# Stages of the last two images issued beside the mixture ahead of each, in a four-layer scan and attention kernel

## The chip, the cores and the metric

The kernel runs on one core of a Trainium2 chip. A core has five engines with queues of their own: TensorE (PE, matmuls into PSUM), VectorE (DVE), ScalarE (ACT, table functions), GpSimd (POOL) and SyncE (SP, which issues DMAs). Each engine takes its instructions in the order in which the program emitted them. The metric is device time in microseconds: 6460.27 as the median of three runs, from 6456.73 to 6466.56.

## The reference

Input and output are four images of 1024 tokens with 256 channels, in float32. Four layers follow each other:

```python
x = conv_scan_block(x)              # layer 0: projection to 512, 3x3 depthwise conv, gelu,
                                    #   scan with 64 states, layernorm, projection; + x
x = bottleneck_conv(x)              # layer 1: 1x1, grouped 3x3, 1x1; relu(out + x)
t = t + graph_attention(_ln_t(t))   # layer 2: masked attention over 1024 tokens, 8 heads,
t = t + moe2(_ln_t(t))              #   mixture of 8 experts, top 2, hidden 256
t = t + scan_block(_ln_t(t))        # layer 3: scan with 16 states over 512 channels,
t = t + moe3(_ln_t(t))              #   mixture of 8 experts, top 2, hidden 512
```

The scan is `h[t] = exp(dt[t] * A) * h[t-1] + dt[t] * x[t] * B[t]`, `y[t] = sum over states of C[t] * h[t]`, for each channel and state, along the 1024 tokens of an image. In both mixtures every expert is computed for every token and weighted by a coefficient that is zero for six of the eight.

## The kernel before

Eight scans (layer 0 or 3, image 0 to 3) run one after the other in the order of `SCANS`: (0,0), (0,1), (3,0), (0,2), (3,1), (0,3), (3,2), (3,3). A scan is cut into units of 128 rows of (state, channel) by 1024 tokens: 256 units for a scan of layer 0, 64 for one of layer 3. One unit is made by `scans`: a DMA of the step sizes dt, spread over the states (`load`, tile dA); `exp(A dt)` on ACT in place (`decay`); two bf16 matmuls that spread the input, held as three bf16 parts in tile S, over the states (`first`, ps_rep); on VectorE a product with the row B and `tensor_tensor_scan`; on POOL a product with the row C; and for each pair of units four matmuls that sum over the states (`pair`, ps_y), which are copied and stored once for 64 channels. A scan's 512 channels are four groups d of 128; each has its own tile S, fetched by `chunk` about `AHEAD = 12` units before its first unit.

All else is in stages that are generators: `front` (layer 0 up to its scan), `middle` (rest of layer 0, layer 1, attention, `moe(2)`, and `front3`, which is layer 3 up to its scan), and `last` (`back3`, which is layer 3 behind its scan, and `moe(3)`). A stage yields a cost after each small step. `run` advances the scans by half a unit and then, with a clock per engine that adds up modelled costs, takes up to `TICKS = 2` steps of the current stage for as long as no engine's clock is ahead of VectorE's. So the two are interleaved in every engine's queue, in an order that is fixed when the program is written. Stages run one at a time, in the order of `STAGES`; `last` of image 2 comes after `middle` of image 3. A stage that needs a scan's result yields a `Wait`, and is taken up again when that group's y store has been emitted.

If the channels of the coming scan are not ready, `chunks_ahead` holds the scan back: with `LATEST = 5` units to go it calls `need`, which advances the stages and nothing else until they are. This happens ahead of scan (3,3), whose input comes from `middle` of image 3: four units of scan (3,2) are then still to be emitted.

The parts of a scan's input come from `steps`: a projection (ps_dt), softplus on ACT (Abs, Exp, Identity, Ln), a sum and a product, a split into three bf16 parts, and stores of dt and parts to DRAM, from where `load` and `chunk` fetch them. For the first scan of the kernel alone it takes another way, with `between`: two projections and softplus first, some other work, and then sums on VectorE, with the parts written from SBUF to S directly (`parts_direct`).

`moe` loads the weights of expert 0, normalizes, transposes, computes router logits (ps_lg), softmax and top 2 (`route`), adds the second bias (ps_b), and then pipes through blocks of one expert and 512 tokens: a group of matmuls ps_h for each 128 hidden channels, Gelu on ACT into h_m, two groups ps_e, and a multiply-add on VectorE into the residual tb. `pipe` issues the later step of one item ahead of the first step of the next. Three PSUM buffers go around for all stages (`ps`): a group waits until the reader of the group three before it is done. `back3` fetches the residual, the gate and y, multiplies y by the gate on POOL, and projects it (ps_o). `pipe`, and all engine calls inside `run`, are recorded at line 128, so that most rows of the profile carry L128.

Of the kernel before, what the change touches and what calls it, by code (L numbers as in the profile page):

```python
# [7 lines left out]
F32 = mybir.dt.float32  # L8
BF16 = mybir.dt.bfloat16
# [7 lines left out]
P = 128  # L17
NB = 4
L = 1024
TB = L // P  # L20
C = 256
# [3 lines left out]
NEXP = 8  # L25
# [16 lines left out]
AHEAD = 12  # L42
LATEST = 5


# [87 lines left out]
class Wait(tuple):  # L133
    pass


class Hybrid:
# [240 lines left out]
    def scans(self, mp, psum):  # L378
# [9 lines left out]
        for scan in SCANS:  # L388
            G = P // self.states[scan[0]]
            units += [  # L390
                (scan, d, c, i, j)
                for d in range(DC) for c in range(2) for i in range(32 // G) for j in range(2)
            ]
        chunks, rows, waiting = {}, {}, []
        state = {}
        self.scan_psum = psum
        y = None

        def load_rows(scan):
            bct, n = self.mem["bc", *scan], self.states[scan[0]]  # L400
            pair = []
            for t in range(2):
                x = mp.tile([P, L], F32, tag=f"rows{t}", name=f"rows{t}", bufs=2)
                nc.sync.dma_start(
                    x, bct[t * n : (t + 1) * n, :].unsqueeze(1).to_broadcast([n, P // n, L])
                )
                pair.append(x)
            rows[scan] = pair

        self.direct = mp.tile([3 * 32, 4, L], BF16, tag="S", name="S", bufs=2)  # L410

# [9 lines left out]
        def chunk(k):  # L421

            if k >= len(units):
                return
            scan, d, c, i, j = units[k]
            if (c, i, j) != (0, 0, 0):
                return
            self.need(scan, d)
            S = self.direct if k == 0 else mp.tile([3 * 32, 4, L], BF16, tag="S", name="S", bufs=2)
            if k == 0:  # L430
                parts_direct(range(1, 4), nc.sync)
            elif d == 0:
                load_rows(scan)
            if k:
                for s in range(3):
                    nc.sync.dma_start(
                        S[32 * s : 32 * s + 32, :, :],
                        self.mem["parts", *scan, d][s].rearrange("(j p) t -> p j t", p=32),
                    )
            chunks[scan, d] = S  # L440

        def chunks_ahead(k, late=False):

            if not late and k + AHEAD < len(units) and units[k + AHEAD][2:] == (0, 0, 0):
                waiting.append(k + AHEAD)
            while waiting:
                scan, d = units[waiting[0]][:2]
                if ("parts", *scan, d) not in self.ready:  # L450
                    if waiting[0] - k > LATEST:
                        break
                    if not late:
                        return True
                    self.alone = True
                chunk(waiting.pop(0))
                self.alone = False
            return False

        def load(k):  # L460
            if k >= len(units):
                return
            scan, d, c, i, j = units[k]
            n = self.states[scan[0]]
            G = P // n
            a = mp.tile([P, L], F32, tag="dA", name="dA", bufs=5)
            r = 64 * c + 32 * j + G * i
            nc.sync.dma_start(
                a, self.mem["dt", *scan, d][r : r + G, :].unsqueeze(0).to_broadcast([n, G, L])
            )  # L470
            state[k] = a

        def decay(k):
            if k >= len(units):
                return
            scan, d, c, i, j = units[k]
# [6 lines left out]
        def first(k):  # L483
            if k >= len(units):
                return
# [38 lines left out]

        self.load, self.load_rows, self.parts_direct = load, load_rows, parts_direct
        for k in range(AHEAD):
            chunk(k)
        for k in range(2, 4):
            load(k)
        decay(0)  # L530
        decay(1)
        first(0)
        for k in range(len(units) + 4):
            waits = chunks_ahead(k)
            load(k + 4)
            if not waits:
                first(k + 1)
            decay(k + 2)
            if k < len(units):
                a, inp = state.pop(k)  # L540
                B, Cm = rows[units[k][0]]
                nc.vector.tensor_tensor(inp, inp, B, ALU.mult)
            yield
            if k < len(units):
                h = mp.tile([P, L], F32, tag="h", name="h", bufs=5)
                nc.vector.tensor_tensor_scan(h, a, inp, 0.0, ALU.mult, ALU.add)
                nc.gpsimd.tensor_tensor(h, h, Cm, ALU.mult)
                state[k] = h
            if k % 2 == 1 and 2 <= k < len(units) + 2:
                pair(k - 2)  # L550
            if waits:
                chunks_ahead(k, True)
                first(k + 1)
            yield
# [68 lines left out]
    def steps(self, fp, key, w, src, chunks, bias, u, between=None):  # L623
# [65 lines left out]
        if between is not None:  # L689
# [6 lines left out]
            yield from between  # L696
            self.load_rows(key)
            for item in ahead:
                add(item, nc.vector)
            for item in ahead:  # L700
                split(item)
            self.load(0)
            self.load(1)
            for item in ahead:
# [876 lines left out]

    def moe(self, which, b, tb):

# [5 lines left out]
        KH = hidden // P  # L1589
        with tc.tile_pool(name=f"m{which}{b}", bufs=1, side="right") as op:  # L1590
            xT = op.tile([P, 2, L], F32, name="xTm")
            cw = op.tile([P, TB, NEXP], F32, name="cw")

# [6 lines left out]

            weights = {0: expert_weights(0)}
            with tc.tile_pool(name=f"mg{which}{b}", bufs=1, side="right") as gp:
                xn = gp.tile([P, TB, C], F32, name="xnm")
# [51 lines left out]
                yield from self.pipe(range(TB // 2), last, add, cost=1.0)  # L1655

            hidden_of = {}
            got = {}
# [105 lines left out]
    def front3(self, b, tb):  # L1764
# [3 lines left out]
        with tc.tile_pool(name=f"g{b}", bufs=1, side="right") as op:  # L1768
# [76 lines left out]
            with tc.tile_pool(name=f"gc{b}", bufs=1, side="right") as fp:  # L1845
                bct = fp.tile([2 * N, L], F32, name="bct3")

                def low(g):
# [6 lines left out]
                nc.sync.dma_start(self.keep(("bc", *key), [2 * N, L]), bct)  # L1855
                yield from self.steps(
                    fp, key, lambda k, d: w_dt[:, k, d * P : (d + 1) * P], u, DC,
                    vec["L3_attn_b_dt"], u,
                )

    def back3(self, b, tb):
        nc, tc = self.nc, self.tc
        with tc.tile_pool(name=f"h{b}", bufs=1, side="right") as sp:
            nc.sync.dma_start(tb, self.mem["t", b])
# [82 lines left out]
    def middle(self, b):  # L1947

        with self.tc.tile_pool(name=f"t{b}", bufs=1, side="right") as tp:
# [3 lines left out]
            yield from self.attention(b, tb)  # L1953
            yield from self.moe(2, b, tb)
            yield from self.front3(b, tb)

    def last(self, b):
        with self.tc.tile_pool(name=f"e{b}", bufs=1, side="right") as tp:
            tb = tp.tile([P, TB, C], F32, name="tb")
# [47 lines left out]
```

## Time and profile before

| | us |
|---|---|
| median of three runs | 6460.27 |
| profiled execution, as timed | 6467.21 |
| its span, first to last instruction | 6465.4 |
| PE busy | 5210.1 (81%) |
| DVE busy | 5153.1 (80%) |
| ACT busy | 3408.1 (53%) |
| POOL busy | 3648.4 (56%) |

Busy time is a sum over the execution; the forty slices and a table of stretches show where it lies. PE's end times are modelled. A row of a group of instructions gives its output and inputs by tile name, the shapes, the count, the busy time in us, the mean of one in ns, and the idle time of its engine just before it with what ended that. The chain of waits goes back from the last instruction to what released each, and its shares show what set the end. The granted PE clock was 0.825 of full speed over the whole span.

### The profile page before, as it was taken

What the parts mean: (1) busy time and instruction counts of PE and PEld (TensorE: products, weight loads), DVE (VectorE), ACT (ScalarE), POOL (GpSimd) and SP (SyncE); (2) the same over time, 40 slices, a digit from 0 to 9 for tenths busy, and PEclk for the clock granted to TensorE, in tenths of its full rate; (3) what the DMA queues carried; (4) which work ended last, traced back from release to release, by engine and by line L of the source; (5) the groups of instructions that cost most, each with busy time, mean ns of one, the idle gap of its engine ahead of it and who ended that gap; (6) DMA issues with size and microseconds to landing.
All of it is one profiled execution on the core that took longest, in us unless ns stands there. A gap on an engine that the chain in (4) does not pass through costs nothing. (4 is left out here: it accounts for less than half of the span.)

```text
span 6465.4 us, 59678 instructions
## 1 busy us (share of the span) xinstructions
PE 5210.1 (81%) x20249; PEld 2107.8 (33%) x20249; DVE 5153.1 (80%) x4328; ACT 3408.1 (53%) x4075; POOL 3648.4 (56%) x1796
## 2 busy tenths in 40 slices
PE   6677685689797579989689689798699688968979
PEld 2222130222342022243245232253254222524656
DVE  5888989988898998899889988898899981258311
ACT  3565664355576335567568445477387353246311
POOL 2797868665557666555856665557756661065100
PEclk7677695689797579989789689798699788978979
DMA  3555546443355566345644665354555750156221
GB/s 114 162 158 174 176 154 198 158 147 116 125 182 174 169 163 163 114 137 178 193 150 165 189 158 142 107 168 163 178 169 168 193 146 7 53 154 159 64 69 33
DMA packets 347995, 935.77 MB, mean 145 GB/s; under 512 B 37444, under 2 KB 119952, under 8 KB 346064
## 3 DMA queue, kind: packets, MB, share of 16 engines
q1 hardware_dynamic: 345248, 929.36, 47.2%
q0 software_dynamic: 2128, 2.13, 0.2%
q8 instruction: 166, 2.72, 0.2%
q14 instruction: 165, 1.35, 0.1%
q10 hardware_dynamic: 288, 0.20, 0.0%
HBM read 841.81 MB, written 93.16 MB: 145 GB/s over the span
## 5 line engine op out<-in xcount | busy, mean ns | idle before, releaser
L128 POOL TENSOR_TENSOR h<-h,rows 128x1024 f32<-128x1024 f32 x1280 | 3026.7, 2367 | 1816.9 <-DVE h L128 1567.0
L128 DVE TENSOR_TENSOR_SCAN h<-dA,ps_rep 128x1024 f32<-128x1024 f32 x1280 | 2923.0, 2284 | 142.8 <-ACT dA L128 12.8
L128 DVE TENSOR_TENSOR ps_rep<-ps_rep,rows 128x1024 f32<-128x1024 f32 x1280 | 1550.9, 1212 | 182.6 <-PE ps_rep L128 178.4
L128 ACT ACTIVATE dA<-dA,A_L_conv_A_log 128x1024 f32<-128x1024 f32 x1024 | 1147.7, 1144 | 616.5 <-DMA dA<-dt 575.9
L128 PE MATMUL ps_rep<-S,spread_L_conv_A_log 96*128 96x512 bf16 x2048 | 770.4, 465 | 840.8 <-DVE h L128 791.1
L128 PE MATMUL ps_y<-h,collect_L_conv_A_log 128*32 128x512 f32 x4096 | 739.5, 773 | 14.6 <-POOL h L128 14.6
L128 PE MATMUL ps_h<-xTm,we 128*128 128x512 f32 x1536 | 716.5, 606 | 0.0
L128 PE MATMUL ps_e<-we,h_m 128*128 128x256 f32 x3072 | 701.2, 381 | 2.5 <-ACT h_m L128 1.7
L128 PEld LDWEIGHTS <-spread_L_conv_A_log 96*128 96x128 bf16 x2048 | 159.3, 103 | 1651.4 <-DVE h L128 1348.1
L128 ACT ACT_TABLE_LOAD x483 | 619.7, 1283 | 58.4 <-PE ps_h L128 43.1
L128 PEld LDWEIGHTS ps_e<-we,h_m 128*128 128x128 f32 x3072 | 579.2, 190 | 153.6 <-issue 62.7
L128 DVE SCALAR_TENSOR_TENSOR tb<-ps_e,cw,tb 128x256 f32<-128x256 f32 x512 | 220.1, 474 | 410.6 <-PE ps_e L128 410.5
L128 ACT ACTIVATE h_m<-ps_h,cols 128x512 f32<-128x512 f32 x384 | 260.2, 687 | 507.7 <-PE ps_h L128 505.2
L128 ACT ACTIVATE p<-ps_sc 128x512 f32<-128x512 f32 x432 | 234.4, 595 | 382.8 <-PE ps_sc L128 381.9
L128 PEld LDWEIGHTS ps_h<-xTm,we 128*128 128x128 f32 x1536 | 292.4, 193 | 333.4 <-issue 287.8
L128 ACT ACTIVATE dA<-dA,A_L_attn_A_log 128x1024 f32<-128x1024 f32 x256 | 290.6, 1146 | 198.3 <-DMA dA<-dt 168.8
L128 PE MATMUL ps_rep<-S,spread_L_attn_A_log 96*128 96x512 bf16 x512 | 182.7, 444 | 178.6 <-DVE h L128 167.7
L128 PE MATMUL ps_at<-p,v 128*32 128x512 f32 x1024 | 276.6, 621 | 0.9 <-ACT sums L128 0.7
L128 PE MATMUL ps_at<-p,ones 128*32 128x512 f32 x1024 | 276.5, 620 | 0.0
L128 PE MATMUL ps_sc<-qT,kT 32*128 32x512 f32 x864 | 262.6, 665 | 14.8 <-ACTq L1382 8.8
L128 POOL TENSOR_TENSOR sp_l<-sp_l,sp_e 128x512 f32<-128x512 f32 x62 | 78.4, 1265 | 272.4 <-DVE sp_e L128 250.5
L128 PE MATMUL ps_cv<-pad,diag 128*128 128x512 f32 x504 | 230.9, 599 | 0.0
(333 smaller groups left out, 4926.2 us busy)
## 6 DMA issues: line engine op xcount, KB each, us to landing
dA<-dt SPq DMA_DIRECT2D x1280, 512.0 KB
we<-in_L_ffn_W_dram SPq DMA_DIRECT2D x64, 512.0 KB
parts<-parts SPq DMA_DIRECT2D x62, 384.0 KB
S<-parts SPq DMA_DIRECT2D x93, 256.0 KB
dt<-sp_r SPq DMA_DIRECT2D x64, 256.0 KB
y<-yo SPq DMA_DIRECT2D x128, 128.0 KB
y_back<-y SPq DMA_DIRECT2D x64, 256.0 KB
we<-in_L_ffn_w_dram SPq DMA_DIRECT2D x64, 256.0 KB
```

Source lines behind the costliest of these rows:

```text
L128: return got(*args, **kw)
```

## The change

1. The list of units gets `DRAIN = 4` empty units ahead of the last scan, and for that scan `chunks_ahead` holds back only with one unit to go. So all of scan (3,2), stores included, is emitted before `need` is called. Loads and decays are counted by `upto`, which stops at a unit whose parts are not fetched.
2. `middle` of image 3 creates `ahead(2)`, that is `back3(2)` and `moe(3, 2)` up to its router, in pools on the left side of SBUF. `beside` takes one step of it after each step of `moe(2, 3)`; `rest` runs what is left up to the marker `END`.
3. In `front3` of image 3, `steps` takes the way with `between`, which is here `BETWEEN = 8` steps of image 2's experts; their first weights are loaded at that point (`begin` of `moe`). The parts of the last scan's first channel group go directly into S, and two loads of dt and the rows are issued ahead. When that group is ready, `beside` adds a step of image 2's experts after each step of the other three groups.
4. `last(2)` runs the rest of image 2's experts with `ahead(3)` beside it, one step each; steps that wait for the last scan are left out until their group is done. `last(3)` is what remains, its expert weights again loaded behind the router.
5. B and C rows are one tile of two halves. Image 2's residual uses one of its buffers, its transposed tokens use the tile of image 0's input, and the bct of front3 of image 3 uses the tile of layer 0's input weights.

```diff
+DRAIN = 4
+BETWEEN = 8
...
+        final = next(k for k, unit in enumerate(units) if unit[0] == SCANS[-1])
+        units[final:final] = [None] * DRAIN
+        final += DRAIN
...
-            S = self.direct if k == 0 else mp.tile([3 * 32, 4, L], BF16, tag="S", name="S", bufs=2)
-            if k == 0:
+            if k in (0, final):
+                S = self.direct
                 parts_direct(range(1, 4), nc.sync)
...
-                    if waiting[0] - k > LATEST:
+                    if waiting[0] - k > (1 if waiting[0] == final else LATEST):
...
+        def upto(what, one, k):
+            while ahead[what] <= k:
+                to = unit(ahead[what])
+                if to and to[:2] not in chunks:
+                    break
+                if to:
+                    one(ahead[what])
+                ahead[what] += 1
...
-            load(k + 4)
+            upto("load", load, k + 4)
...
-            self.load_rows(key)
+            self.begin(key)
...
-            self.load(0)
-            self.load(1)
+            self.two_loads()
...
+            if pause:
+                yield END
+                begin()
...
-                    vec["L3_attn_b_dt"], u,
+                    vec["L3_attn_b_dt"], u, self.some(self.other, BETWEEN) if last else None,
                 )
+                if last:
+                    steps = self.beside(steps, self.other, lambda: ("parts", *key, 0) in self.ready)
+                yield from steps
...
-            yield from self.moe(2, b, tb)
+            moe = self.moe(2, b, tb)
+            if b < NB - 1:
+                yield from moe
+            else:
+                self.other = self.ahead(b - 1, "left", self.scan_pool)
+                yield from self.rest((yield from self.beside(moe, self.other)))
             yield from self.front3(b, tb)
...
+    def beside(self, main, other, begin=lambda: True):
+
+        held = None
+        for cost in main:
+            yield cost
+            if other is None or not begin() or (held and held not in self.done):
+                continue
+            held = None
+            more = next(other, END)
+            if more is END:
+                other = None
+            elif isinstance(more, Wait):
+                held = tuple(more)
+            else:
+                yield more
+        if held:
+            yield Wait(held)
+        return other
...
+    def ahead(self, b, side, pool=None):
+
+        with ExitStack() as stack:
+            if pool is None:
+                pool = stack.enter_context(self.tc.tile_pool(name=f"e{b}", bufs=2, side=side))
+            tb = pool.tile([P, TB, C], F32, tag="rows", name="tb_rows", bufs=2 if pool is self.scan_pool else 1)
+            yield from self.back3(b, tb, side)
+            yield from self.moe(3, b, tb, side, True)
+            self.nc.sync.dma_start(self.image(self.out, b), tb)
+            yield 1.0
+
     def last(self, b):
+        if b == NB - 2:
+            self.other, before = self.ahead(b + 1, "right"), self.other
+            yield from self.beside(before, self.other)
+            return
+        if b == NB - 1:
+            for more in self.other:
+                if more is not END:
+                    yield more
+            return
```

## The prediction

> **What bounds the kernel now.** I read the page's forty slices first, then a table of stages, then the chain of waits.
>
> ```profile
> PE   6677685689797579989689689798699688968979
> DVE  5888989988898998899889988898899981258311
> GB/s 114 162 158 174 176 154 198 158 147 116 125 182 174 169 163 163 114 137 178 193 150 165 189 158 142 107 168 163 178 169 168 193 146 7 53 154 159 64 69 33
> ```
>
> For 33 slices VectorE is 8 to 9 tenths busy: the scans set the pace, and the change leaves them alone there. It acts on the last seven slices, where VectorE falls to 1 or 2: first image 3 finishes its middle stages with no scan beside it, then the last scan runs, then two images finish one after the other. Cut at the trace's own borders (columns: stretch, length, then busy time and count of PE, weight loads, DVE, ACT, POOL, then clock, DMA share, GB/s):
>
> ```profile
> 5330.00:5467.00 137.00, 127.14 (x712) 35.34 (x704) 19.18 (x35) 55.69 (x67) 11.20 (x8) 0.97 0.03 8
> 5467.00:5504.00 37.00, 20.33 (x71) 15.96 (x72) 12.60 (x50) 12.79 (x23) 9.96 (x8) 0.50 0.03 10
> 5504.00:5618.00 114.00, 113.41 (x386) 73.79 (x385) 28.39 (x65) 23.27 (x33) 0.00 (x0) 0.98 0.10 28
> 5618.00:5693.00 75.00, 67.85 (x160) 29.39 (x160) 5.30 (x23) 25.12 (x40) 0.00 (x0) 0.93 0.23 85
> 5693.00:5751.00 58.00, 38.99 (x93) 14.49 (x92) 24.71 (x22) 45.00 (x65) 39.41 (x29) 0.82 0.46 125
> 5751.00:5897.00 146.00, 92.04 (x318) 36.25 (x319) 126.97 (x115) 51.24 (x61) 97.58 (x51) 0.60 0.75 193
> 5897.00:6027.00 130.00, 128.38 (x511) 66.74 (x510) 120.50 (x90) 106.22 (x103) 75.45 (x32) 0.98 0.64 161
> 6027.00:6159.00 132.00, 130.59 (x467) 86.95 (x465) 17.37 (x40) 25.81 (x37) 2.34 (x1) 1.00 0.09 26
> 6159.00:6236.00 77.00, 39.40 (x136) 30.14 (x136) 14.57 (x50) 9.36 (x18) 14.80 (x12) 0.60 0.38 116
> 6236.00:6465.00 229.00, 222.67 (x770) 146.48 (x768) 28.71 (x65) 43.97 (x64) 0.00 (x0) 0.98 0.10 33
> ```
>
> In order: rest of attention (image 3); router of its mixture 2; its experts; front3; the softplus steps with four left-over units of scan (3,2); scan (3,3) beside back3 and router of image 2; the scan beside image 2's experts; their rest alone; back3 and router of image 3 alone; its experts alone. Experts are dense PE work at full clock (222 us an image), so they can only be hidden by filling PE time that is idle elsewhere: 5467 to 5504, 5693 to 5897, and 6159 to 6236. The last of these, in the chain of waits:
>
> ```profile
> 6159.57 4.44 DMA out_dram<-tb
> 6166.26 8.09 DMA w_L_attn_W_out<-in_L_attn_W_out_dram
> 6174.36 10.45 DMA y_back<-y
> 6187.21 15.11 PE ps_o L128 x58
> 6215.35 6.64 PE ps_lg L128 x32
> ```
>
> Output, loads and small steps in a row: latency, not work.
>
> **The change part by part.** I add up the stages again, against the span of 6465.4 us of the profiled execution (6467.2 us as timed).
>
> *Drained scan.* Four empty units and a limit of 1 instead of 5 put the four left-over units of scan (3,2) beside attention. Each costs PE about 1.13 us (two ps_rep and half a pair of ps_y: 0.60 and 0.53 us in the timeline at full clock), and PE is full there (127 of 137 us): +5, stage 142. Without that place they would still cost four times 3.5 us of VectorE ahead of the last scan, as they do now. Empty units issue nothing.
>
> *back3 and router of image 2 beside mixture 2 of image 3.* Moved: 64 ps_o matmuls, 16 transposes, 32 ps_lg, 8 ps_ct, 16 ps_b. From the row of the same work alone, PE 15.1 + 5.5 + 6.8 + 1.9 + 7.1 = 36. On POOL, twelve products and sums of 1.26 us go past mixture 2's four residual sums, and POOL is idle there otherwise. On SP, 14 loads at about 0.5 us of issue (7 us) go past expert weights that are fetched a block ahead. The alternation is one to one: mixture 2's router has 34 steps and back3 about 33 without PE work, so router time is not filled with PE work; the 36 us come beside the experts. There every moved PE step waits in PE's own order for ACT or DVE, with one expert step (1.72 us) as cover. Stalls: 0 to 68 us (68 moved steps, at most 1 us each); I take 8. Stage: 37 + 114 + 36 + 8 = 195 in place of 151.
>
> One rule speaks against this. The Trainium skill, "ScalarE: Activation LUTs", Table sets, says to do all activations of one table set before switching. Mixing Ln and Exp of one image with Gelu of another adds about 4 loads here and some 13 in the last scan's softplus. Its rules for authors budget about 2.7 us a switch; this trace has
>
> ```profile
> L128 ACT ACT_TABLE_LOAD x483 | 619.7, 1283 | 58.4 <-PE ps_h L128 43.1
> ```
>
> 1.283 us (as the page's section on the load itself has it). ACT works 0.69 of every 1.72 us of an expert step, which leaves 1.03: a load overruns it by 0.25 us at 1.28 and by 1.7 at 2.7. For 17 switches that is 4 us by the row (inside the 8) against 29 by the rule's budget. I take the row.
>
> *Edits without a price.* B and C rows in one tile are the same two loads. Image 2's residual takes the row buffer that scan (0,3) left, its transposed tokens and front3's bct take tiles that only the fronts read: all long free. If one were not, back3 of image 2 would start late, which is the half-kept rival below.
>
> *front3* stays 75 us: nothing runs beside it until the softplus.
>
> *Start of the last scan.* From the first ps_dt matmul now, 58 us pass to the first (3,3) unit. New: two projections end at 7.4; softplus on ACT at 13.9. Eight expert steps stand between, and their weights are only issued here (1 MB in all; rows range from 4.4 us for the 1 MB output to 8.1 us for 0.5 MB of W_out in a crowd). Their second and third matmul groups need the PSUM buffers that the softplus holds until VectorE has read them (about 15), so the eighth group ends near 26 and the seventh Gelu near 25. Only then, in ACT's order, come the casts of the parts, and behind them the direct DMAs of channel group 0 and the first decays; without the eight steps the casts could start at 17. The first scan of the kernel takes the same direct path: cast 108.50, first ps_rep 117.85, its product done at 120.2. So 25 + 12 = 37. That scan then waits for 18 direct loads, which keep SP 12.2 us ahead of the dA loads: its fifth unit is about 10 us late. Here dA loads of two units are out earlier; I take 5. Stage: 42 instead of 58, with 14 us of experts done in it.
>
> *The last scan.* 64 units took 146 + 130 = 276 us. Beside experts the trace shows 26 units in 99.7 us, 3.83 us each, in a stage whose PE is 98.8% busy; the softplus of the other three channel groups costs VectorE about 5 more. 64 x 3.83 + 5 = 250. PE in it: 250 less 64 x 1.13 for the scan, less 22 for six projections (3.65 each), less 4: 152 us of experts. SP also carries image 3's gate and y loads; a y load waits for its store, and dA loads queue behind it. The same mixture runs today at 5751 to 5897, where ACT waits 50.3 us for dA but VectorE only 1.6 us for ACT: nothing.
>
> The second rule, "TensorE: Matmul & The Clock Gate", Part 1, says that PE falls to half clock after an idle window of about 3.4 us and stays there about as long. The stages agree that sparse ones get 0.50 to 0.82. By the rule each gap costs 1.7 us more; the new order has perhaps four, 7 us. By the row none is added to the scan, as its 3.83 was seen at clock 0.98. I add none and keep 7 in the range.
>
> *After the scan.* Experts left: 222 - 14 - 152 = 56, and image 3's projection beside them, 15: 71 in place of 132. There are 25 expert steps left against some 41 steps of image 3, so its router from the normalization on is uncovered: 27 us (6209 to 6236), and the weights, now fetched only after it, 6 (4 to 8): 33 in place of 77. Then 229 as before.
>
> **Sum:** 142 + 195 + 75 + 42 + 250 + 71 + 33 + 229 = 1037, against 1135: -98. Span 6367; on the median of the runs shown, 6460 - 98 = **6362 us**, 1.5% less.
>
> **Rivals.** *Denser:* no stall beside mixture 2 (-8), the scan start without its 5, cadence at the 3.6 us of the whole stage 5897 to 6027 with PE still full, and the router of image 3 covered in half (-17): about 6325. For it: PE is the bound in the whole tail. Against: alternation ignores who is late.
>
> *Half kept:* the moved steps stall PE as they stall the scan today (28 units took 146 us where 3.83 each makes 107, so 39 us over about 70 steps); 0.5 us for each of 68 steps, and the router of image 3 left alone in full (+15): about 6415. This is also where it ends if image 2's stages find their scan unfinished and run only after mixture 2.
>
> *Slower:* PE takes its matmuls in order, so a step of the other image whose operand is late stops the expert matmuls behind it. About 125 steps are interleaved (68, 16, 41). From 0.9 us of stall for each beyond what I counted the gain is gone; at 1.1 us the time is about 6490. For it: 0.6 us a step is what the scan loses today. Against: in the tail ACT, DVE and POOL are mostly idle, and each step has 1.7 us of cover.
>
> **How the numbers follow.** Chances: mine 0.55, denser 0.17, half kept 0.21, slower 0.07. The measurement can tell about 0.2% (13 us) from no change. Faster: the first three but for 0.01, 0.92; slower 0.06; same 0.02. Range: 6312 (denser, less the 13 us of noise) to 6425 (half kept with the clock gaps); the likeliest case alone holds 6335 to 6390.
>
> **What would show it.** Right: in a table by stage, no stretch of the last 1100 us with PE under 0.8 but the router of mixture 2, the scan's start and some 30 us before the last experts; the mixture stage near 195; 64 scan units in about 250; about 56 us of expert work between scan and image 3. Wrong: PE waits for ACT or POOL inside mixture 2 above 30 us, a scan cadence above 4.2, or a DMA wait of PE for expert weights above 10 us.

## The result, and the profile after

The changed kernel takes **6377.88 us** (median of four runs, 6372.08 to 6380.72), against 6462.40 for the kernel before beside it: a ratio of 0.9869, with a 95% interval of 0.9854 to 0.9885. It is 1.3% faster. That is 16 us above the 6362 that were predicted (a gain of 84.5 us in place of 98); the time lies in the range given, and in the likeliest case's own (6335 to 6390).

The forty slices of the changed kernel, to be laid beside those of the prediction:

```profile
PE   6677685689797568979789779888689689797999
DVE  5888999988898998889889998899989985216811
```

The last slices of PE read 7999 where they read 8979. VectorE's dense part behind the gap reads 68 where it read 583: the four left-over units of scan (3,2) no longer stand at its head. The table of stretches, cut at the same borders of the work (columns as in the prediction):

```profile
5323.00:5464.00 141.00, 130.83 (x742) 36.65 (x734) 32.92 (x44) 58.21 (x73) 20.67 (x12) 0.98 0.03 9
5464.00:5506.00 42.00, 21.33 (x73) 16.32 (x74) 16.81 (x49) 12.80 (x23) 24.66 (x20) 0.51 0.51 145
5506.00:5649.00 143.00, 140.45 (x520) 96.46 (x520) 42.62 (x114) 35.95 (x54) 0.00 (x0) 0.97 0.08 23
5649.00:5724.00 75.00, 68.11 (x160) 29.33 (x160) 5.13 (x23) 25.13 (x40) 0.00 (x0) 0.93 0.23 85
5724.00:5760.00 36.00, 25.36 (x55) 10.49 (x55) 9.31 (x13) 19.36 (x27) 0.00 (x0) 0.88 0.53 151
5760.00:6044.00 284.00, 252.15 (x954) 130.34 (x953) 242.77 (x184) 213.11 (x224) 188.10 (x95) 0.95 0.73 181
...
6044.00:6113.00 69.00, 69.00 (x273) 50.37 (x272) 13.52 (x33) 10.11 (x14) 7.30 (x5) 1.00 0.09 27
6113.00:6149.00 36.00, 21.75 (x75) 16.22 (x74) 10.37 (x37) 8.09 (x17) 0.00 (x0) 0.55 0.15 49
6149.00:6379.00 230.00, 222.94 (x768) 146.81 (x768) 28.02 (x64) 45.25 (x65) 0.00 (x0) 0.98 0.12 38
```

Against the sum of the prediction:

| stage | before | predicted | measured |
|---|---|---|---|
| rest of attention | 137 | 142 | 141 |
| mixture 2 of image 3 (router, experts) | 151 | 195 | 185 |
| front3 | 75 | 75 | 75 |
| start of the last scan | 58 | 42 | 36 |
| last scan | 276 | 250 | **284** |
| experts and projection behind it | 132 | 71 | 69 |
| router of image 3 alone | 77 | 33 | 36 |
| experts of image 3 | 229 | 229 | 230 |
| sum | 1135 | 1037 | 1056 |

Seven stages are within 10 us, and one is off by 34: the last scan was to become 26 us shorter and became 8 longer. The tail gained 79 us. The two profiled spans differ by 86 (6465.4 and 6379.0); the other 7 lie ahead of attention of image 3, in code that the change leaves alone, and a second execution of the changed kernel lies 7 us later there too, so this is no part of the gain.

The chain of waits, where it had three DMAs in a row and 15 us of ps_o ahead of the last router:

```profile
6092.92 3.45 PE ps_o L130 x16
6101.84 14.59 issue
6124.20 6.64 PE ps_lg L130 x32
6137.99 7.13 PE ps_b L130 x16
6145.24 4.11 DMA we<-in_L_ffn_W_dram
```

The projection now lies among experts, and what is left is the router, then a wait for the expert weights that are fetched only behind it. ACT's table loads (the row that the prediction shows) went from 483 to

```profile
L130 ACT ACT_TABLE_LOAD x508 | 651.8, 1283 | 91.2 <-PE ps_h L130 58.8 <-DMA dA<-dt 20.5 <-DMA S<-parts 3.4
```

**Where the scan's 34 us are.** VectorE's rows by group, first before the change (5693 to 5755, the softplus ahead of the last scan), then after it (5760 to 6044, the whole of that scan; all waits of sp_x and sp_e lie in its first 92 us):

```profile
L128 DVE TENSOR_TENSOR sp_x<-sp_l,parts 128x512 f32<-128x512 f32 x7 | 7.9, 1134 | 24.7 <-ACT parts L128 24.7
```

```profile
L130 DVE TENSOR_TENSOR_SCAN h<-dA,ps_rep 128x1024 f32<-128x1024 f32 x64 | 146.2, 2285 | 12.8 <-ACT dA L130 6.9 <-DVE ps_rep L130 0.5
L130 DVE TENSOR_TENSOR ps_rep<-ps_rep,rows 128x1024 f32<-128x1024 f32 x64 | 77.6, 1212 | 5.8 <-PE ps_rep L130 5.8
L130 DVE SCALAR_TENSOR_TENSOR tb_rows<-ps_e,cw,tb_rows 128x256 f32<-128x256 f32 x44 | 18.9, 472 | 3.2 <-PE ps_e L130 3.2
L130 DVE TENSOR_TENSOR sp_x<-sp_l,parts 128x512 f32<-128x512 f32 x6 | 5.3, 876 | 21.9 <-ACT parts L130 21.9
L130 DVE SCALAR_TENSOR_TENSOR sp_e<-ps_dt,sp_e 128x512 f32<-128x512 f32 x6 | 4.1, 684 | 2.1 <-ACT sp_l L130 2.1
```

The numbers behind the last bar are VectorE's idle time just before the row and what ended it. In both kernels VectorE waits five times, at a half of a channel group each, for a cast on ACT: 4.7 to 5.0 us before, 2.4 to 6.2 after. Before, these waits passed ahead of the first unit of (3,3), as a part of the 58 us of its start. Now the scan starts after one group, and the waits for the other three are inside the scan. One of them, in the timeline of ACT and then of VectorE (start, duration, engine, work, idle before it):

```profile
5778.12 2.18 ACT L130 ACTIVATE dA<-dA,A_L_attn_A_log 128x1024 f32<-128x1024 f32 x2
5781.96 0.69 ACT L130 ACTIVATE sp_r<-ps_dt,cols 128x512 f32<-128x512 f32 x1 [1.66 <-PE ps_dt L130]
5782.55 0.68 ACT L130 ACTIVATE sp_e<-ps_dt,cols 128x512 f32<-128x512 f32 x1
5783.24 1.28 ACT L271 ACT_TABLE_LOAD   x1
5784.54 0.63 ACT L130 ACTIVATE sp_e<-sp_e 128x512 f32<-128x512 f32 x1
5785.20 0.60 ACT L130 ACTIVATE ps_dt<-sp_e 128x512 f32<-128x512 f32 x1
5785.83 0.60 ACT L130 ACTIVATE sp_l<-ps_dt 128x512 f32<-128x512 f32 x1
5786.32 2.17 ACT L130 ACTIVATE dA<-dA,A_L_attn_A_log 128x1024 f32<-128x1024 f32 x2
5788.40 0.61 ACT L130 CAST parts<-sp_l 128x512 bf16<-128x512 f32 x1
```

```profile
5783.16 1.22 DVE L130 TENSOR_TENSOR ps_rep<-ps_rep,rows 128x1024 f32<-128x1024 f32 x1
5789.04 0.69 DVE L130 TENSOR_TENSOR sp_x<-sp_l,parts 128x512 f32<-128x512 f32 x1 [4.66 <-ACT parts L130]
5789.65 0.68 DVE L130 SCALAR_TENSOR_TENSOR sp_e<-ps_dt,sp_e 128x512 f32<-128x512 f32 x1
5790.25 2.28 DVE L130 TENSOR_TENSOR_SCAN h<-dA,ps_rep 128x1024 f32<-128x1024 f32 x1
```

VectorE has made its product at 5784.4 and could scan: that unit's decays ran early enough for it. But sp_x stands ahead of the scan in its order, and the cast that sp_x needs stands on ACT behind the next half's whole softplus and two decays, and that softplus itself waited 1.66 us for a projection on PE. The next scan starts at 5790.25. By the rows, VectorE's time from the first unit to the last adds up so: 223.8 us for the scan's own scans and products, 18.9 for the experts' adds, 9.4 for softplus, 24.0 waiting for ACT at sp_x and sp_e, 6.9 waiting for decays, and some 5 for PE (4.6 of the ps_rep row's 5.8 lie ahead of the first unit). That is 288, as neighbouring rows overlap by some 1%. The first two make 242.7, or 3.79 a unit, against the 3.83 that was predicted.

### The profile page after: what moved, and what is told of

Same layout as the page of the kernel before. It is cut to its first block, busy times and chain, and to the rows that moved or that the text cites. A ratio compares the mean times of both kernels' runs of the same rounds, so it can differ in the third digit from the quotient of the medians.

```text
span 6379.0 us, 59672 instructions
## 1 busy us (share of the span) xinstructions
PE 5170.1 (81%) x20249; PEld 2103.5 (33%) x20249; DVE 5154.0 (81%) x4336; ACT 3437.9 (54%) x4103; POOL 3639.3 (57%) x1788
## 5 line engine op out<-in xcount | busy, mean ns | idle before, releaser
L130 ACT ACT_TABLE_LOAD x508 | 651.8, 1283 | 91.2 <-PE ps_h L130 58.8
L130 PE MATMUL ps_h<-xTm,we 128*128 128x512 f32 x1280 | 596.9, 604 | 4.4 <-DMA we<-in_L_ffn_W_dram 4.4
L130 PEld LDWEIGHTS ps_h<-xTm,we 128*128 128x128 f32 x1280 | 243.0, 193 | 277.8 <-issue 240.3
L130 DVE SCALAR_TENSOR_TENSOR tb_rows<-ps_e,cw,tb_rows 128x256 f32<-128x256 f32 x128 | 55.7, 476 | 244.6 <-PE ps_e L130 244.6
L130 DVE SCALAR_TENSOR_TENSOR tb<-ps_e,cw,tb 128x256 f32<-128x256 f32 x384 | 164.2, 472 | 82.7 <-PE ps_e L130 82.6
```

What stands on the lines that cost most here:

```text
L130: return got(*args, **kw)
```

## The experiments

To compare a few microseconds, the profiled executions are lined up at one unit of scan (3,2), ahead of all that the change touches. The tail runs from it to the end of the last expert matmul. "Start" is from the first ps_dt of front3 to the first unit of (3,3); "scan" from the start of that unit to the start of the last; "rest" from the last unit's end to the last expert matmul of image 2; "gap" from there to image 3's first expert matmul. All are read from the timelines. The kernel before was timed anew beside each set of runs (medians from 6455.6 to 6462.4), and each ratio is to its own. Row 11 has no border to read: image 3's experts begin there among image 2's.

| | start | scan | rest | gap | tail | median us | ratio to before |
|---|---|---|---|---|---|---|---|
| before | 58.0 | 273.9 | 131.2 | 77.8 | 1141.6 | 6462.4 | |
| changed | 36.2 | 281.9 | 69.2 | 35.9 | 1062.6 | 6377.9 | 0.9869 |
| changed, again | 37.0 | 280.8 | 69.3 | 36.0 | 1064.8 | 6379.2 | 0.9870 |
| 1 softplus alone | 38.7 | 267.5 | 99.1 | 22.3 | 1068.8 | 6382.1 | 0.9892 |
| 2 no Gelu table | 35.8 | 268.8 | 69.3 | 35.4 | 1049.0 | 6363.0 | 0.9861 |
| 3 image 3 alone | 36.0 | 277.9 | 55.4 | 80.7 | 1089.7 | 6401.6 | 0.9921 |
| 4 image 2 behind mixture 2 | 35.2 | 281.7 | 69.2 | 35.8 | 1076.5 | 6394.9 | 0.9911 |
| 5 two steps | 36.0 | 283.9 | 78.1 | 10.9 | 1048.5 | 6365.0 | 0.9860 |
| 6 early weights | 36.1 | 284.9 | 69.2 | 31.6 | 1061.8 | 6369.9 | 0.9862 |
| 7 scan behind softplus | 107.6 | 262.1 | 10.7 | 52.6 | 1069.3 | 6387.7 | 0.9898 |
| 8 in twos | 35.2 | 300.9 | 69.3 | 35.7 | 1083.4 | 6392.1 | 0.9899 |
| 9 parts through DRAM | 66.0 | 262.9 | 69.3 | 35.4 | 1072.9 | 6389.2 | 0.9888 |
| 10 = 5 + 6 | 36.0 | 287.2 | 81.5 | 6.3 | 1050.2 | 6366.7 | 0.9853 |
| 11 = 1 + 5 + 6 | 37.9 | 269.6 | | | 1060.8 | 6377.7 | 0.9871 |

Each ratio has an interval of about 0.0016 on either side, 10 us, so the tails carry the finer readings; two executions of the changed kernel differ by 2.2 us in the tail.

The changed kernel again:

> The changed kernel once more, for the same chip and rounds as the three beside it. From the marked unit of scan (3,2) to the last expert matmul 1062.6 us passed in its first profile, with 282 us between the last scan's first and last unit; both within 4 us of that.

**1. No experts beside the softplus** of the last three groups (the experts' pipeline is cut behind the block ahead, so that no PSUM buffer stays held).

```diff
-BETWEEN = 8
+BETWEEN = 9
...
+            cut = 8 if side == "left" else 0
+            if cut:
+                yield from self.pipe(items[:cut], one, two, cost=3.4)
+            yield from self.pipe(items[cut:], one, two, cost=2.6 if which == 2 else 3.4)
...
-                if last:
-                    steps = self.beside(steps, self.other, lambda: ("parts", *key, 0) in self.ready)
```

> The changed kernel without expert steps beside the softplus of the last three channel groups (image 2's experts pause after their first eight matmul groups until the softplus is issued). In the changed kernel the last scan takes 284 us, of which its first 90 us hold about 35 us of lost pace, and VectorE waits 21.9 us there for ACT's casts. Theory A (the experts beside the softplus are the cause: each Gelu brings two table loads, and ps_dt waits for PSUM buffers that Gelus hold): that wait falls under 8 us, the scan takes 255 to 265, the experts left after it rise from 54 to about 75 us, more of image 3's router is covered, and the whole is 0 to 12 us faster than the changed kernel. Theory B (the softplus itself, a chain of ACT, POOL and VectorE in order with the scan's own work, is the cause): the wait stays at 18 or more, the scan stays above 275, and the whole is 10 to 20 us slower than the changed kernel.

Between the two theories in the scan, and outside theory A in the end. The scan is 14 us shorter, and the wait of sp_x for casts 9.9 us in place of 21.9. But 30 us more of experts are left behind it, and the tail is 6 us longer. So more than half of the wait comes with the expert steps, and filling PE there is still worth it.

**2. Identity in place of Gelu in image 2's experts**, which takes as long on ACT (681 and 686 ns).

```diff
-                        hidden_of[e, g][:, i, :], got.pop(item), AF.Gelu,
+                        hidden_of[e, g][:, i, :], got.pop(item), AF.Identity if side == "left" else AF.Gelu,
```

> The changed kernel with Identity in place of Gelu in image 2's last mixture, so that its activations force no table load (it leaves the Gelu of that image out). If the table loads between Exp and Gelu are what slows the start of the last scan (the Trainium skill's rule on grouping by table set), the wait of VectorE for casts falls from 21.9 us to under 10, and the time falls by 20 us or more. If it is the order of the softplus chain in the queues, each Gelu step still stands ahead of a cast: the wait falls only by the loads, some 7 us, and the time by less than 10.

ACT's table loads within the scan, in the changed kernel (two rows) and in this one (one row):

```profile
L130 ACT ACT_TABLE_LOAD x61 | 78.3, 1283 | 16.5 <-DMA dA<-dt 15.6
L271 ACT ACT_TABLE_LOAD x6 | 7.7, 1283 | 0.1
```

```profile
L271 ACT ACT_TABLE_LOAD x6 | 7.7, 1283 | 0.1
```

With 61 loads gone, 78 us of ACT, the scan is 13.1 us shorter and the tail 13.6; the wait of sp_x for casts falls to 12.7. That is between the two forecasts: the loads are a good part of the cost, and the order is the rest. Of the 13, 7.7 come in the first 16 units (92.6 us in the one, 84.9 in the other), where 8 of the loads were: about a microsecond for each there, and 0.1 for each of the other 53. A load costs most of its time only where VectorE waits for ACT.

**3. Image 2's experts first, and image 3's last stages alone behind them.**

```diff
-            self.other, before = self.ahead(b + 1, "right"), self.other
-            yield from self.beside(before, self.other)
+            before, self.other = self.other, None
+            yield from before
+            self.other = self.ahead(b + 1, "right")
             return
```

> The changed kernel with the fourth part undone: image 2's experts are issued alone, and back3 and router of image 3 after them. By the prediction's sum: the projection's 15 us leave the experts' stage, and 77 us stand alone in place of 36 (33 predicted): 26 us slower than the changed kernel, near 6404. If the interleaving stalls PE as much as it hides (the slower rival), the time is the same within 8 us.

The tail is 27 us longer: the gap is 80.7 us, near the 77.8 of the kernel before, so 45 longer; the rest is 14 shorter without the projection, and the scan 4. That part of the sum stands.

The 4 us of the scan are a find of their own. In this run image 3's y and W_out are fetched behind the scan, and VectorE's waits for decays fall from 6.9 us to 2.7:

```profile
L130 DVE TENSOR_TENSOR_SCAN h<-dA,ps_rep 128x1024 f32<-128x1024 f32 x64 | 146.2, 2285 | 9.0 <-ACT dA L130 2.7 <-DVE ps_rep L130 0.5
```

In the changed kernel SP issues a load of dA at 5867.6 us and the next only at 5878.3, with y_back and W_out between them; VectorE's two waits for decays that are missing here come soon after, at 5887 and 5894.

**4. Image 2's last stages behind mixture 2**, not beside it.

```diff
-                yield from self.rest((yield from self.beside(moe, self.other)))
+                yield from moe
+                yield from self.rest(self.other)
```

> The changed kernel with the second part undone in its order alone: back3 and router of image 2 are issued after mixture 2 of image 3 and before its front3, not beside it. By the prediction's sum the stage from the end of attention to front3 goes from 185 us to 151 + 77 = 228, so 43 us slower than the changed kernel, near 6421. If interleaving costs stalls that a serial order doesn't have, the difference is under 25 us.

14 us longer, a third of what I expected, and not for stalls of the interleaved order (beside the experts PE waits 1.8 us in all). Where the kernel before took 77 us for these stages of image 3, here they take 49 behind the mixture: the residual, gate and y came in during the experts, and POOL's products were done, so ps_o starts at once. Over a third of the 77 us was waiting for those. Moving the stages to where their inputs are long there removes that wait by itself; the interleaving adds the step from 49 us to 29.

**5. Two steps of image 3 for each expert step** of image 2.

```diff
             more = next(other, END)
+            if n == 2 and more is not END and not isinstance(more, Wait):
+                yield more
+                more = next(other, END)
...
-            yield from self.beside(before, self.other)
+            yield from self.beside(before, self.other, n=2)
```

> Two steps of image 3 instead of one go in beside each expert step of image 2 behind front3. In the changed kernel 36 us lie between image 2's last expert matmul and image 3's first, with PE busy for 21.8 of them. Theory (image 3's steps come too late for the cover): they are reached under image 2's experts, the 21.8 us of PE work stay and the idle 14 go; about -14 us against the changed kernel (-17 to -8), counted from the same unit of scan (3,2) to the end, and the 36 us fall under 12. Rival (steps asked for earlier have operands that are late, and stop PE in its own order): the 36 us shrink, but the time from the last scan unit to image 2's last expert matmul grows by as much, 0 to +5 us in all.

As the theory has it: -14.1, with a gap of 10.9. PE around the former gap, in the timeline:

```profile
6113.65 3.72 PE L130 MATMUL ps_e<-we,h_m 128*128 128x256 f32 x16
6117.30 1.99 PE L130 MATMUL ps_b<-b,cT 8*128 8x256 f32 x8
6119.99 3.78 PE L130 MATMUL ps_b<-b,cT 8*128 8x256 f32 x8 [0.70 <-DVE tb_rows L130]
6128.27 7.02 PE L130 MATMUL ps_h<-xTm,we 128*128 128x512 f32 x10 [4.51 <-DMA we<-in_L_ffn_W_dram]
```

The router is under the experts but for its last matmuls, and the wait for weights is what remains.

**6. Image 3's expert weights ahead of its router**, as in the kernel before.

```diff
-            yield from self.moe(3, b, tb, side, True)
+            yield from self.moe(3, b, tb, side, side == "left")
```

> Image 3's first expert weights are loaded ahead of its router, as in the kernel before, and not behind it. The changed kernel's PE waits 4.4 us for them. Theory: the wait goes, -4 us (-5 to -3), nothing else moves. Rival: the router's own last step (the coefficients that the experts need) ends just behind the load, and 0 to -1 us is gained.

The gap is 4.3 us shorter, as the theory has it, and the tail only 0.8, for the scan took 3 us longer. The weights are asked for behind the scan, so they can't be the reason, and I have none.

**7. The last scan only when all four groups are ready.**

```diff
-            self.need(scan, d)
+            self.need(scan, DC - 1 if k == final else d)
...
-                if ("parts", *scan, d) not in self.ready:
+                group = DC - 1 if waiting[0] == final else d
+                if ("parts", *scan, group) not in self.ready:
```

> The last scan starts only when all four of its channel groups are ready, so no softplus runs in it; the expert steps beside it stay. In the changed kernel 282 us pass from its first to its last unit. Theory A (the surplus over 250 is the softplus of three groups in the scan's first 90 us: its work on VectorE, its casts behind Gelu and table loads on ACT): 282 becomes 245 to 255, the start comes 35 to 45 us later, and since the surplus was idle time of PE, the end comes earlier by some 10 us (-25 to +5). Rival B (the cadence beside experts is itself above 3.83, from loads of dA behind gates and from PE): 265 or more, and the end 15 us later or more.

Between the two theories. The scan is 20 us shorter without softplus, not 27 to 37. The last 40 units take 153.3 us, 3.83 each: the cadence beside experts is right, and rival B's reason is out. But the first 24 units wait 20.3 us on VectorE, for the decays of the first units (8.1), ps_e (9.6) and ps_rep (2.6): with everything held until the end, the direct parts and the dA loads start at once beside the experts, which may be why; no run takes them apart. And the scan's start is 71 us later, not 40, so image 2's experts run out and image 3's router is bare (52.6). The tail is 6.7 us longer, so starting early is worth that much.

**8. The same expert steps in twos.**

```diff
+            if every > 1 and other is not None and begin():
+                count += 1
+                if count % every == 0:
+                    yield from self.some(other, every)
+                continue
...
-                    steps = self.beside(steps, self.other, lambda: ("parts", *key, 0) in self.ready)
+                    steps = self.beside(steps, self.other, lambda: ("parts", *key, 0) in self.ready, every=2)
```

> During the softplus of the last three channel groups the expert steps come two after every second softplus step instead of one after each; the amount is the same. With Identity in place of Gelu the scan was 13 us shorter. Theory A (it is the number of table loads): the 8 added loads become 4 or 5, and the scan from first to last unit goes from 282 to 276 (274 to 279). Rival B (it is the single Gelu in ACT's order, that waits for its PE group while a cast stands behind it): two in a row wait no less, 280 to 286.

Both miss: the scan is 19 us longer, 301 us. The loads did not become fewer (509 in all, for 508), as decays stand between the softplus steps in any case. The waits of its first 63 us (engine and operation, what it waited for, us in total, times, longest):

```profile
DVE sp_x L130 <- ACT parts L130: 18.3, 3, 8.2
ACT sp_r L130 <- PE ps_dt L130: 13.8, 2, 8.4
...
PEld ps_e L130 <- ACT h_m L130: 8.4, 1, 8.4
```

It is a ring: PE's expert group waits for a Gelu, the projection stands behind that group on PE, the softplus on ACT waits for the projection, the cast stands behind the softplus, and VectorE waits for the cast. But over the whole scan that end of the ring costs VectorE no more than in the changed kernel:

```profile
DVE ps_rep L130 <- PE ps_rep L130: 24.1, 7, 7.6
DVE sp_x L130 <- ACT parts L130: 22.7, 4, 8.2
```

The casts take 22.7 us for 21.9. What grew is the wait for ps_rep, from 5.8 to 24.1: the scan's own matmuls stand behind the expert group too. The longest such wait, 7.6 us, follows a group that waited 8.0 us for its Gelu and then took 6.4 us for 16 matmuls, which take 3.7 in the rows of experiment 5; the granted clock was 0.59 in that group. So the cost of a foreign step is not its table load alone, but what stands behind it in each order.

**9. The first group's parts through DRAM**, and expert steps one by one from the first softplus on.

```diff
-            if k in (0, final):
+            if k == 0:
...
-                    vec["L3_attn_b_dt"], u, self.some(self.other, BETWEEN) if last else None,
+                    vec["L3_attn_b_dt"], u, None,
...
-                    steps = self.beside(steps, self.other, lambda: ("parts", *key, 0) in self.ready)
+                    steps = self.beside(steps, self.other, lambda: True)
```

> The last scan's first channel group takes the common way, parts stored and fetched through DRAM, with no block of eight expert steps; one expert step goes beside each softplus step from the first on. Theory (the direct parts shorten the start): the first unit comes 50 us (44 to 58) after the first projection, not 36, with some 6 expert steps in it and group 1's softplus partly done, so the scan itself takes 270 to 280 and the end comes 10 us later (5 to 18). Rival (the scan's first 90 us are set by the softplus of the other groups, whichever way the first parts come): the later start is given back in the scan, -3 to +3 us.

The end is 10.3 us later, as the theory has it, out of larger terms: the start costs 30 us more (66, where 44 to 58 was expected) and the scan gives back 19 (263, for 270 to 280), since more of the softplus is then done before it. Of the 30 us that the direct parts take from the start, 19 only move into the scan.

**10 and 11. The router's two edits together, and with experiment 1's.**

> Two steps of image 3 beside each expert step of image 2, and image 3's first expert weights loaded ahead of its router. With the first alone the tail was 14.1 us shorter, and PE still waited 4.5 us for the weights just ahead of the last experts. Theory (the two are one after the other on the path): -18 to -19 us against the changed kernel. Rival (the weights ahead of the router crowd the loads of dA, as the scan of the run with early weights alone was 3 us longer): -13 to -15.

> No expert step beside the softplus of the last three groups, and the two edits of image 3's router. Without those expert steps the scan was 14 us shorter and the tail 6 us longer. Theory (the expert work left over is dense PE work behind the scan, and the router of image 3 is under it either way): the scan 266 to 270, and -6 us (-12 to 0) against the changed kernel, so worse than the two router edits alone. Rival (the router was all that the shorter scan still waited for): -20 us or better.

Ten: -12.4 us against the first execution of the changed kernel, -14.6 against the second; the gap is down to 6.3, but the scan is again 5 to 6 us longer, so the weights' 4 us do not show in the end; that is the rival's forecast, not the theory's. Timed together, its median is 6366.71 (6363.64 to 6367.73), against 6379.17 (6372.10 to 6389.99) for the changed kernel, with ratios to the kernel before of 0.9853 (0.9837 to 0.9870) and 0.9870 (0.9854 to 0.9887). These intervals overlap, the runs' times and the tails don't. Five alone is as good in the tail, and either is the version to keep. Eleven: -1.8, inside the theory's -12 to 0. With the router covered, a shorter scan still buys nothing, since its experts are left to do behind it.

## Why the prediction was right and wrong

**The sign and the bulk were right by their steps.** In the tail PE is the bound where experts can fill it: the rest of experts (71 predicted, 69 measured), the bare router (33, 36), the drained units (+5, +4) are as summed, and experiment 3 gives the 27 us of image 3's stages back when they are put alone.

**The step that failed** is "the softplus of the other three channel groups costs VectorE about 5 more". It counted VectorE's work (9.4 us as measured) and not its waits for ACT's casts: 24.0 us. That is 28 us too little of the 34, and the decays' waits of 6.9 us are the rest. For 2.7 of these, in the first units, I had put 5 into the start. The other 4 come behind image 3's loads, which stand on SP ahead of loads of dA: I had named that queue and put it at "nothing", and experiment 3, without them, has a scan 3 to 4 us shorter than the two executions of the changed kernel. The sign of being wrong that I had named, a cadence above 4.2, is there (284 us for 64 units are 4.4), but not from the cadence beside experts. The "24.7 <-ACT parts" was in the trace of before. I took the 16 us of a shorter start from it, and did not ask where the waits that had filled that start would go: with the scan begun early they became the scan's. Experiments 1 and 2 show how they are made up: the 21.9 us at sp_x fall to 9.9 us without the expert steps, and to 12.7 without the Gelu's table loads.

That the time still fell into the likeliest case is in part luck: with the scan's 34 us alone it would have been 6396, outside 6335 to 6390. Errors of the other sign, 10 in the mixture stage, 6 in the start and 2 behind the scan, took half of it back.

**The rivals** rested on a miscount. I gave 28 units of the last scan to the 146 us beside back3 and 36 to the 130 us beside experts. The rows of the kernel before, in these two stretches, have 31 and 33:

```profile
L128 DVE TENSOR_TENSOR_SCAN h<-dA,ps_rep 128x1024 f32<-128x1024 f32 x31 | 70.8, 2283 | 4.0 <-ACT dA L128 1.6
L128 DVE TENSOR_TENSOR_SCAN h<-dA,ps_rep 128x1024 f32<-128x1024 f32 x33 | 75.4, 2284 | 3.3
```

So the stage beside experts ran at 3.9 us a unit and not at the 3.6 of "denser", and "half kept" loses 27 us over its 70 steps, 0.4 each and not 0.6, which puts it nearer 6404. "Slower" loses the whole gain at 98 / 125 = 0.8 us a step, not 0.9. My own 3.83, read from the last 26 units, was not touched by this. "Half kept" also took its stall from image 2's back3 beside the scan; beside the experts PE now waits 1.8 us in all. "Slower" named the right mechanism, a late operand in an in-order engine, but for PE beside the mixtures, and it appeared on VectorE in the scan.

**The switches of table sets.** I took 4 us for 17 added loads (25 came, 483 to 508), and kept them under the 8 us of mixture 2's stalls, with "some 13 in the last scan's softplus" hidden by idle ACT. Experiment 2 shows 13 us in the scan for all 61 loads between Gelu and the scan's Exp, 8 of them in the softplus. The trace's 1283 ns was the right price of a load. But 1.03 us of spare ACT beside an expert step is no cover where the next step of another chain stands behind it. The Trainium skill's rule ("ScalarE: Activation LUTs", Table sets) to do all of one set before switching was the better guide to the place, though not by the 2.7 us that the page's "Rules for kernel authors" budget: the dearest loads here cost a microsecond. Experiment 8 is no test of the rule, as its loads did not become fewer; it shows that putting Gelus together can lose 19 us by order alone.

**The mixture stage** ended 10 us below. PE waits once in its experts, 1.8 us for a Gelu, where I allowed 8; the loads of image 2 lie in the router's 42 us (DMA share 0.51), and PE waits for none of the tiles that the edits share. The experts' stretch grew by 29 us (143 less 114), not by the 36 that the moved work costs alone. PE's rows by group, alone before the change (6159 to 6236), then beside experts after it (5506 to 5649):

```profile
L128 PE MATMUL ps_b<-b,cT 8*128 8x256 f32 x16 | 7.2, 639 | 0.0
L128 PE MATMUL ps_lg<-wr,xTm 128*128 128x8 f32 x32 | 6.8, 357 | 0.0
L128 PE MATMUL ps_tr<-ident,xnm 128*128 128x128 f32 x16 | 5.5, 448 | 7.5 <-ACT xnm L128 7.4
```

```profile
L130 PE MATMUL ps_lg<-wr,x 128*128 128x8 f32 x32 | 4.6, 284 | 0.0
L130 PE MATMUL ps_b<-b,cT 8*128 8x256 f32 x16 | 4.5, 400 | 0.0
L130 PE MATMUL ps_tr<-ident,xnm 128*128 128x128 f32 x16 | 2.4, 272 | 0.0
```

The granted clock is 0.60 in the one stretch and 0.97 in the other. I used the row of a sparse stretch for work that was moved into a dense one. The rule of "TensorE: Matmul & The Clock Gate", Part 1, which I had weighed, by an estimate from its idle window, as a loss of 7 us for new gaps, worked the other way: moved out of a sparse stretch, the matmuls of these rows are 8 us cheaper (19.5 and 11.5). In experiment 4, where they run alone again, they take 7.2, 6.8 and 5.5.

**The start** ended 6 below: casts of the parts at 25.6 us behind the first projection, the first unit at 36.2, as "25 + 12 = 37" has it. The 5 us for late dA loads are not in it; what there is of them lies in the scan.

## What to carry to other kernels

When a chain is started earlier, list the waits that filled the time ahead of it, and say in which engine's order they will stand then: such a wait is not gone, it can stand inside the stage and stop the engine that sets the pace. Price moved work by a row from where it is going, not from where it comes from. And when two streams are interleaved one to one, see which of them runs out: two for one at the end was worth 14 us, where the three other ways of mixing beside the softplus (experiments 1, 8 and 9) each lost 6 to 21.

## What the hardware showed that I had not expected

A table load of 1283 ns cost about a microsecond where VectorE waited for ACT, and a tenth of that elsewhere in the same scan. Thirty-two 8-wide matmuls of the router took 6.64 us alone and 4.43 among experts, in the chains of before and after. Sixteen expert matmuls behind an idle 8.0 us of PE took 6.4 us in place of 3.7. And experiment 6 lengthened the scan by 3 us without an instruction moved in it; in experiment 10, 5 to 6 us longer, y and W_out of image 3 are also fetched up to 6 us earlier in the scan. Against a spread of 1 us between two executions of the changed kernel both stay open.
